# Giving out the first part of the last "back" between the last steps of the scans

## Chip, cores and metric

The program runs on one core of one Trainium2 chip. The time is the device time of that core in microseconds (us); lower is better. Three timed runs of the kernel before gave 13518.94, 13519.48 and 13551.32 us, so the median is 13519.48 us.

## What is computed

The input is a batch of 8 images of 64 channels and 64 x 64 positions, all in fp32. Four layers follow each other: an attention over all 4096 positions, two shifted-window attention blocks with their MLPs, a layer of position-dependent 3 x 3 filters with a convolution, and a state-space layer with four scan directions. Only the last layer bears on this change. Cut to what matters:

```
y  = out_y[:, 0] + inv[:, 0] + wh + invwh          # sum of the four scan directions
y  = _ln(y, outnorm_g, outnorm_b) * silu(z)        # over 128 inner channels
xh = xh + einsum("bhwd,cd->bhwc", y, outproj_w) + outproj_b
n  = _channel_ln(xh, cn_g, cn_b)
xo = xh + gelu(aggr(four dwconvs of n, three of them max-pooled by 2, 4, 8)) * n
```

Each direction is a recurrence over 4096 positions, `h = h * exp(dt * A) + dt * B * u`, for 128 channels and 16 states, followed by the sum over states of `h * C`.

## The kernel before

The images go through in four pairs, p = 0 to 3. `front(p)` computes the first three layers of a pair and the inputs of its scans and leaves them in DRAM. `scans(p)` (L1657) computes the scans, with the sums of the four directions written to DRAM. `back(p)` (L1808) reads these sums and does the rest of the last layer. `front` and `back` are Python generators: each `yield` gives up a piece of work with a cost. While `scans(p)` is written out step by step, it draws pieces of `back(p - 1)` and `front(p + 1)` in between, so these lie beside the scans. For the last pair, p = 3, only `back(2)` is left to lie beside its scans, and `back(3)` itself is run after everything, at L1930.

**The scans.** `scans` splits the work of a pair into 64 units: 2 images, 4 directions in the order k = 1, 3, 0, 2, and 8 blocks of 512 positions. A unit has 8 steps of two states each, so a pair has n = 512 steps. In step i, SP fetches B and C rows for later steps (`fetch`, L1720, 512 KB each, three buffers of each), POOL multiplies B by `dt * u` into `v` (`products`, L1725), ACT computes `exp(dt * A)` into a PSUM bank `dad` (L1747), DVE runs the two scans (L1750), and DVE or POOL multiply by C (L1765). For the last pair one of the two states of a step has its scan output left in PSUM and its C product done on DVE, in every fourth step both. PE adds the products into a PSUM bank with identity matmuls (`sums`, L1789). After the eighth step the bank is added into Y (L1799, L1801) and, in the fourth direction of an image, DVE forms the final sum of this block (L1804) and SP writes it to DRAM, tile `ys` (L1805). The fourth direction goes backward: its blocks are c = 7, 6, ..., 0. The tile of the final sum is the unit's own input tile `xs`, of which there are two, so the load of a later `xs` (L1697) waits for such a write.

**The back.** Its first part is a loop over the same blocks in the same order, c = 7 to 0, with three yields in each:

```python
for c in reversed(range(NCH)):
    po = self.bank("po3")
    for im in range(2):
        # load y (ys of this image) and z; normalise y:
        pc, sd = self.normed(...)          # PE pc, ACT square, PE pv, ACT ln, ACT exp
        # DVE u = pc * g * sd ; DVE u = (u + b) * z ; PE po[half] = opT @ u
        yield 6
    # DVE X = po + bias + X ; normed(X) ; DVE F = pc * g * sd ; ACT F = F + b
    yield 6
```

These are L1816 to L1833, with `normed` at L1231 to L1243. The two images share the partitions, so a block needs the sums of both: those of image 6 are finished halfway through the scans of p = 3, those of image 7 only in their last 8 units. The second part (from L1845) max-pools the whole of F three times, and then does the convolutions, the gelu and the output by blocks of 8 image rows. It needs all eight blocks of F.

**What sets the order.** Every engine has its own instruction queue, and the tile framework orders the instructions when it builds the program: it takes them by their place in the program text as soon as they can go, and gives buffers out in that order. PSUM banks come from two groups of three, "f" and "da". When `back(2)` has been used up during the last scans, `turn` is set (L1683), and from then on `bank` (L1209) alternates between the two groups for every request: the exponentials of the scans and the pieces of `back(3)` share all six.

Of the kernel before, what the change touches and what calls it, by code (L numbers as in the profile page):

```python
# [15 lines left out]
B, C, HH, WW = 8, 64, 64, 64  # L16
# [9 lines left out]
NTD = L // TD  # L26
# [1131 lines left out]
class _Direct:  # L1158
# [498 lines left out]
    def scans(self, p, beside, cost):  # L1657

        self.units = []
        for im in range(2):
            out = self.memory("ys")
            self.kept["y", 2 * p + im] = out
            for nth, k in enumerate((1, 3, 0, 2)):
                order = range(NTD) if k < 2 else range(NTD - 1, -1, -1)
                self.units += [dict(image=2 * p + im, k=k, c=c, at=at, nth=nth, out=out) for at, c in enumerate(order)]
        self.inputs(self.units[0])
        n = 8 * len(self.units)
        steps = [{} for _ in range(n)]  # L1670
        done = 0
        for i in range(-3, n):
            if i + 3 < n:
                self.fetch(i + 3, steps[i + 3], 0)
            if 0 <= i + 2 < n:
                self.fetch(i + 2, steps[i + 2], 1)
                self.products(i + 2, steps[i + 2])
            if i >= 0:
                self.step(i, steps[i])
                if i:  # L1680
                    self.sums(i - 1, steps[i - 1], steps[i]["w"])
                if p == B // 2 - 1 and done >= cost:
                    self.turn = max(self.turn, 0)  # L1683
                while done < cost * (i + 1) / (n - LEAD):
                    done += next(beside, cost)
            if i % 8 == 1 and i // 8 + 1 < len(self.units):
                self.inputs(self.units[i // 8 + 1])
        self.sums(n - 1, steps[n - 1])
        self.run(beside)

    def inputs(self, u):

        nc, w, net = self.nc, self.w, self.net
        wk, ps = self.sw, self.ps
        k, c = u["k"], u["c"]
        x = u["x"] = wk.tile([P, TD], F32, name="xs", tag="xs")
        nc.sync.dma_start(x, self.kept[u["image"]][k % 2][:, c * TD : (c + 1) * TD])  # L1697

        pd = ps.tile([P, TD], F32, name="pdd", tag="da")
        nc.tensor.matmul(pd, lhsT=net.xdt[:, k, :], rhs=x, start=True, stop=True)  # L1700
        du = u["du"] = wk.tile([P, 2, TD], F32, name="du", tag="du")
        nc.scalar.activation(
            pd, pd, AF.Exp, bias=w["dtb"][:, k : k + 1], accum_out=net.esum[:, u["image"], k, c : c + 1]
        )
        nc.scalar.activation(pd, pd, AF.Ln, bias=1.0)
        nc.vector.tensor_tensor(du[:, 1], pd, x, ALU.mult)
        nc.scalar.activation(du[:, 0], pd, AF.Copy)
        pb = ps.tile([2 * NST, TD], F32, name="pbc", tag="da")
        nc.tensor.matmul(pb, lhsT=w["xbc"][:, k, :], rhs=x, start=True, stop=True)
        bc = wk.tile([2 * NST, TD], F32, name="bc", tag="bc")  # L1710
        nc.scalar.activation(bc, pb, AF.Copy)
        rows = u["rows"] = self.dram.tile([2 * NST, TD], F32, name="rows", tag="rows")
        nc.sync.dma_start(rows, bc)
# [198 lines left out]
@with_exitstack  # L1912
def tile_kernel(ctx: ExitStack, tc: tile.TileContext, x: bass.AP, packs, layout, out: bass.AP):
    net = _Net(ctx, tc, x, packs, layout, out)
    with ExitStack() as path:
        net.open(path, True)
        d = _Direct(net, path)
        net.log_exp()
        front, first = d.begin(path)
        back = 0.25 * front  # L1920
        for p in range(B // 2):
            works, cost = [], 0
            if p:
                works.append(d.back(p - 1))
                cost += back
            if p + 1 < B // 2:
                works.append(d.front(p + 1))
                cost += front if p else front - first
            d.scans(p, d.chain(*works), cost)
        d.run(d.back(B // 2 - 1))  # L1930

    with tc.tile_pool(name="check", bufs=1) as pool:
        bad = net.in_range(pool)
    with tc.If(bad > 0), ExitStack() as path:
        net.open(path, False)
        for p in range(B // 2):
            t = net.layer0(p)
            t = net.layer1(t)
            t = net.layer2(t)
            net.layer3(t, p)  # L1940
# [21 lines left out]
```

## Time and profile before

| | us |
|---|---|
| median of three timed runs | 13519.48 |
| the profiled execution's own time | 13549.57 |
| its span | 13547.6 |
| the last pair's fourth direction of image 7: first and last final sum (L1804) | 13054.7 and 13293.1 |
| `back(2)`'s first part: first and last step of F (L1832) | 10957 and 11439 |

The profile is of one execution. It lies 30.1 us above the median, about where the slowest of the timed runs lies (13551.32 us). Sums are made against this execution and then set against the median. The span is 1.97 us shorter than the time of the execution; nothing in that remainder is touched. "Busy" in a table of stretches is the time in which at least one instruction of the engine ran, so instructions that overlap by a tenth of a microsecond are not counted twice. A wait is put down to whatever came last.

### The profile page before, as it was taken

To read this page: it belongs to the slowest core of one execution; us is meant where nothing else is said; L and a number is where in the kernel's file an instruction comes from. 1 tells how busy PE (TensorE), PEld (TensorE's weight loads), DVE (VectorE), ACT (ScalarE), POOL (GpSimd) and SP (SyncE) were. 2 spreads that over 40 slices of the span, in tenths; PEclk is the share of its full clock that TensorE was granted. 3 is DMA by queue.
4 is the path that set the end of the run, shared out by engine and by line. 5 is a ranking of instruction groups with operands and counts; after the bars stand their busy time and mean duration, and the time that the engine had idled before them with its cause. 6 is when DMAs were issued, how large, how long until landed. Compare 5 with 4: busy or idle time off the path is not lost. (4 is left out here: it accounts for less than half of the span.)

```text
span 13547.6 us, 140341 instructions
## 1 busy us (share of the span) xinstructions
PE 10802.4 (80%) x45762; PEld 3981.2 (29%) x45762; DVE 8783.4 (65%) x10407; ACT 7087.6 (52%) x15569; POOL 7764.9 (57%) x3875
## 2 busy tenths in 40 slices
PE   9999986888787669989888667997898666666665
PEld 2243322333232222224432222223443222222221
DVE  0121236776668676676666767667675768988985
ACT  5556514564545646655554545665653644544542
POOL 0000004887778764466666685446675687777881
PEclk9999977998898779999889788998888788888887
DMA  0000004776667765455555674455554677787882
GB/s 24 1 1 1 3 13 170 238 238 211 207 218 244 235 200 168 155 186 175 169 178 175 221 250 168 158 167 176 186 192 151 209 241 262 235 280 264 303 283 86
DMA packets 706249, 2385.12 MB, mean 176 GB/s; under 512 B 81120, under 2 KB 81248, under 8 KB 704480
## 3 DMA queue, kind: packets, MB, share of 16 engines
q1 hardware_dynamic: 681312, 2319.76, 50.9%
q10 hardware_dynamic: 24192, 56.29, 1.1%
q8 instruction: 362, 5.93, 0.2%
q14 instruction: 383, 3.14, 0.1%
HBM read 2272.97 MB, written 102.76 MB: 175 GB/s over the span
## 5 line engine op out<-in xcount | busy, mean ns | idle before, releaser
L1725 POOL TENSOR_TENSOR vd<-B,du 128x1024 f32<-128x1024 f32 x2048 | 4832.8, 2367 | 3924.8 <-DMA B<-rows 2573.0
L1789 PE MATMUL yd<-vd,pack 128*128 128x512 f32 x7540 | 4263.8, 696 | 1381.0 <-POOL vd L1761 591.9
L1747 ACT ACTIVATE dad<-du,As 128x512 f32<-128x512 f32 x4096 | 2729.0, 681 | 1130.8 <-DVE hd L1750 684.1
L1750 DVE TENSOR_TENSOR_SCAN hd<-dad,carry,vd 128x512 f32<-128x512 f32 x2166 | 2713.2, 1270 | 677.8 <-ACT dad L1747 385.9
L1789 PEld LDWEIGHTS yd<-vd,pack 128*128 128x128 f32 x7540 | 1497.0, 215 | 3843.5 <-issue 1654.4
L1761 POOL TENSOR_TENSOR vd<-hd,C 128x1024 f32<-128x1024 f32 x658 | 1551.4, 2358 | 1068.2 <-DVE hd L1750 702.0
L1750 DVE TENSOR_TENSOR_SCAN dad<-dad,carry,vd 128x512 f32<-128x512 f32 x1418 | 1793.3, 1274 | 160.3 <-POOL vd L1725 99.1
L1765 POOL TENSOR_TENSOR vd<-hd,C 128x512 f32<-128x512 f32 x1154 | 1476.1, 1280 | 512.5 <-DVE hd L1750 446.4
L1313 ACT ACTIVATE e<-s 128x512 f32<-128x512 f32 x2048 | 1200.7, 591 | 751.1 <-PE s L1307 749.6
L1307 PE MATMUL s<-X 64*128 64x512 f32 x4096 | 1344.4, 646 | 30.5 <-ACT e L1313 28.8
L1299 PE MATMUL po<-e,VT 128*64 128x512 f32 x4096 | 1226.7, 621 | 12.6 <-ACT e L1313 9.9
L1765 DVE TENSOR_TENSOR vd<-dad,C 128x512 f32<-128x512 f32 x1300 | 864.9, 672 | 48.2 <-ACT carry L1758 39.1
L1758 ACT ACTIVATE carry<-hd 128x1 f32<-128x1 f32 (+1 forms) x1586 | 317.3, 201 | 920.3 <-DVE hd L1750 917.0
L1758 ACT ACTIVATE carry<-dad 128x1 f32<-128x1 f32 x1422 | 240.9, 169 | 804.1 <-DVE dad L1750 801.4
L1307 PEld LDWEIGHTS s<-X 64*128 64x128 f32 x4096 | 375.9, 186 | 915.2 <-issue 783.1
L1447 DVE TENSOR_TENSOR w_e<-w_s,bias 128x512 f32<-128x512 f32 x512 | 329.9, 681 | 424.3 <-PE w_s L1435 423.6
L1462 PEld LDWEIGHTS w_av<-vals,w_e 64*64 64x64 f32 x16384 | 546.7, 144 | 197.3 <-issue 86.8
L1462 PE MATMUL w_av<-vals,w_e 64*64 64x9 f32 x16384 | 574.9, 207 | 30.4 <-ACT w_e L1452 30.1
L1700 PE MATMUL pdd<-xs,xdt 128*128 128x512 f32 x512 | 348.3, 768 | 257.8 <-DMA xs<-xc 121.4
L1452 ACT ACTIVATE w_e<-w_e 128x512 f32<-128x512 f32 x512 | 311.8, 626 | 366.9 <-DVE w_e L1447 251.6
L1299 PEld LDWEIGHTS po<-e,VT 128*64 128x64 f32 x4096 | 236.1, 135 | 847.5 <-issue 763.9
L1574 PE MATMUL acc<-tap,pack 128*128 128x512 f32 x576 | 367.5, 761 | 99.5 <-DVE tap L1573 98.1
(252 smaller groups left out, 11129.2 us busy)
## 6 DMA issues: line engine op xcount, KB each, us to landing
B<-rows SPq DMA_DIRECT2D x2048, 512.0 KB, 5.2
C<-rows SPq DMA_DIRECT2D x2048, 512.0 KB, 4.6
xs<-xt SPq DMA_DIRECT2D x128, 256.0 KB, 3.5
xs<-xc SPq DMA_DIRECT2D x128, 256.0 KB, 4.2
xc<-xcv ACTq DMA_DIRECT2D x64, 256.0 KB, 4.0
zs<-z ACTq DMA_DIRECT2D x64, 256.0 KB, 3.7
xt<-XT ACTq DMA_DIRECT2D x32, 512.0 KB, 7.8
rows<-bc SPq DMA_DIRECT2D x256, 64.0 KB, 1.6
```

The lines of the kernel that those rows point to most:

```text
L1299: nc.tensor.matmul(po[half[im]], lhsT=VT[:, t, half[im]], rhs=es[im], start=(t == 0), stop=(t == 31))
L1307: nc.tensor.matmul(ss[im], lhsT=at(half[im], t), rhs=X[half[im], jc * CH : (jc + 1) * CH], start=True, stop=True)
L1313: nc.scalar.activation(e, ss[im], AF.Exp, scale=C**-0.5, accum_out=parts[:, im, t, jc : jc + 1])
L1462: nc.tensor.matmul(self.av[half[im], x % 4 + j, h, :], lhsT=es[h // 4][half[im], j, h % 4, :], rhs=V[half[im], x + j, h, :], start=True, s ...
L1574: nc.tensor.matmul(acc, lhsT=w["ident"], rhs=tap, start=(t == 0), stop=(t == TAPS - 1))
L1725: self.nc.gpsimd.tensor_tensor(v, st["B"], dx.to_broadcast([P, 2, TD]), ALU.mult)
L1747: nc.scalar.activation(da, u["du"][:, 0], AF.Exp, scale=net.As[:, k, n : n + 1])
L1750: nc.vector.tensor_tensor_scan(along(to), along(da), along(v[:, j]), first, ALU.mult, ALU.add)
L1758: nc.scalar.activation(cs, ends, AF.Copy)
L1761: st["w"] = nc.gpsimd.tensor_tensor(v, h, CC, ALU.mult)
L1765: m = engine.tensor_tensor(v[:, j], hs[j], CC[:, j], ALU.mult)
L1789: m = nc.tensor.matmul(u["y"], lhsT=w["ident"], rhs=v, start=start, stop=stop)
```

## The change

`scans` makes the generator of `back(3)` itself, when it is at the last pair, and draws one piece of it after steps 3, 5 and 7 of every unit among the last seven (n - 8 * 7 = 456, so i = 459, 461, 463, ..., 511: 21 pieces, three for each of blocks c = 7 to 1). What is left of it, block c = 0 and the whole second part, runs after the last sum, as all of it did before. The call in `tile_kernel` goes away.

```diff
@@ in scans
         self.inputs(self.units[0])
         n = 8 * len(self.units)
+
+        late = self.back(p) if p == B // 2 - 1 else None
         steps = [{} for _ in range(n)]
@@
                 while done < cost * (i + 1) / (n - LEAD):
                     done += next(beside, cost)
+            if late and i >= n - 8 * (NTD - 1) and i % 8 in (3, 5, 7):
+                next(late)
             if i % 8 == 1 and i // 8 + 1 < len(self.units):
                 self.inputs(self.units[i // 8 + 1])
         self.sums(n - 1, steps[n - 1])
         self.run(beside)
+        if late:
+            self.run(late)
@@ in tile_kernel
             d.scans(p, d.chain(*works), cost)
-        d.run(d.back(B // 2 - 1))
```

Block c of image 7 is written one unit before the first piece of this block is drawn: unit c = 7 ends with i = 455, its final sum is written out with i = 456, and the pieces of block 7 come at i = 459, 461 and 463. No instruction is added or taken away: the number on each engine is the same, and so is everything computed.

## The prediction

> **What bounds the kernel now.** I read the table of stretches first, for the last two groups of units and for what follows them (columns: stretch, length, busy us and instructions of PE, PEld, DVE, ACT, POOL, clock, DMA share, GB/s).
>
> ```profile
> 12545.00:13005.00 460.00, 316.06 (x577) 106.63 (x576) 423.93 (x449) 235.50 (x561) 415.72 (x225) 0.90 0.88 304
> 13055.00:13285.00 230.00, 137.89 (x237) 45.32 (x238) 178.79 (x191) 96.99 (x229) 173.07 (x94) 0.85 0.72 257
> 13294.00:13458.00 164.00, 99.17 (x124) 26.90 (x122) 36.41 (x57) 48.70 (x79) 0.00 (x0) 0.66 0.14 45
> 13458.00:13547.60 89.60, 37.75 (x66) 15.01 (x66) 78.69 (x125) 16.07 (x22) 0.00 (x0) 0.69 0.07 25
> ```
>
> Row 1, other directions of image 7: DVE is busy 92% and POOL 90%. Row 2, the last direction: DVE is down to 78%, so there is room. Row 3, the last back's first part: PE 60%, ACT 30%, DVE 22%, POOL nothing. No engine is full there; the waits of this stretch tell why:
>
> ```profile
> PEld po L1827 <- DVE u L1826: 66.6, 16, 4.6
> ACT n_sd L1242 <- PE pv L1240: 66.4, 24, 6.7
> DVE u L1825 <- ACT n_sd L1243: 60.5, 16, 5.5
> DVE F L1832 <- ACT n_sd L1243: 50.5, 8, 6.3
> ```
>
> PE waits for DVE, ACT for PE, DVE for ACT, in turn: one dependent chain per block, 8 blocks. The timeline gives its start, the chain of waits its end:
>
> ```profile
> 13293.14 0.69 DVE L1804 TENSOR_TENSOR xs<-Y,yd 128x512 f32<-128x512 f32 x1 [2.63 <-PE yd L1789]
> 13293.86 0.32 SPq L1805 DMA_DIRECT2D ys<-xs  x1
> ...
> 13453.08 2.09 PE pv L1240 x2
> 13456.58 0.76 DVE F L1832
> 13458.12 2.29 DVE big L1845
> ```
>
> From the end of the last final sum, 13293.83, to the first instruction of the second part, 13458.12, it is 164.3 us.
>
> **What the Trainium skill says.** "PSUM — Partial Sum Buffer", section "Engine vs sequencer instructions": the queues of ScalarE, VectorE and GpSimd are strictly first in, first out, and matmuls go in program order. So a moved instruction that isn't ready holds up the scans queued behind it. The trace agrees: 60.5 us of DVE waiting stand at the head of its queue for L1825 alone. "SBUF — State Buffer", section "SBUF: two separate sides": a DVE operation with two SBUF inputs and a GpSimd operation exclude each other for the whole instruction. Of the back's DVE work only L1826 (u and z) is of that kind. The trace agrees, see its two durations below. "DMA: Bandwidth & Descriptors", section "Two DMAs through the same engine are not ordered": the reader of what a DMA wrote must wait for its semaphore before it is issued; the last block pays this below.
>
> **The change, part by part.**
>
> *Removed from the end.* Seven of the eight blocks leave it. What remains is block 0 after the last sum. Its chain, from the durations around 13304 us and the landings of the table of DMA issues: final sum ends 13293.8; ys write 2.0; yb read 2.7, with 0.3 for the two issues, 5.0; pc 2.1, square 0.6, pv 2.1, ln 0.7, exp 0.6, two u 1.5, po 1.4, X 0.75: 9.75; pc 2.1, square 0.6, pv 2.1, ln and exp 1.3, F 0.75, bias 0.7: 7.55. With hand-overs, some 0.1 at each of 15 steps, 1.5. Sum 23.8, taken as 24. Image 6's half of the block is ready early and hides beside it. The end becomes 164.3 − 24 = 140.3 us shorter. Block 1, whose last piece is written after the last step, must also be through; its ys lands one unit earlier, so I count nothing for it. The second part (89.6 us) is the same, only earlier.
>
> *Added to the last seven units.* The final sums go from 13054.7 to 13293.1, 238.4 us in 7 units, so 34.06 us each. Of block work each unit gets: PE 99.17 / 8 = 12.4 us (at a clock of 0.66; less at 0.85), ACT 48.70 / 8 = 6.1, DVE six instructions, SP four loads of 256 KB. What these cost beside scans is seen where `back(2)` lies beside scans, from 10900 to 11440 us:
>
> ```profile
> L1826 DVE SCALAR_TENSOR_TENSOR u<-u,pack,zb 128x512 f32<-128x512 f32 x15 | 21.5, 1433 | 0.2
> L1825 DVE SCALAR_TENSOR_TENSOR u<-pc,pack,n_sd 128x512 f32<-128x512 f32 x15 | 11.1, 738 | 29.8 <-ACT n_sd L1243 29.8
> L1832 DVE SCALAR_TENSOR_TENSOR F<-pc,pack,n_sd 128x512 f32<-128x512 f32 x8 | 5.9, 742 | 14.8 <-ACT n_sd L1243 14.8
> L1829 DVE SCALAR_TENSOR_TENSOR X<-po,pack,X 128x512 f32<-128x512 f32 x8 | 5.9, 739 | 4.0 <-PE po L1827 4.0
> ```
>
> L1826 is 1433 ns here and 752 ns in the end stretch, where POOL is idle. Per block DVE works 2 x 0.74 + 2 x 1.43 + 0.74 + 0.74 = 5.8 us, and waits at the head of its queue (29.8 + 14.8 + 4.0) / 8 = 6.1 us. What DVE has free now:
>
> ```profile
> DVE dad L1750 <- POOL vd L1725: 43.0, 25, 4.0
> DVE hd L1750 <- POOL vd L1725: 8.1, 8, 2.2
> ```
>
> That is 51.1 us in 230, or 7.6 us in a unit, spent waiting for POOL's product. Bounds on the growth of a unit: from below nothing, since 178.79 / 230 x 34.06 = 26.5 us of DVE work and 5.8 make 32.3, less than 34.06 (and less than nothing has no reason, no scan work goes away). From above 5.8 + 6.1 = 11.9 us, if no waiting is shared. In units 0 to 8 of the last pair (first L1706 at 11173.2, ninth at 11440.5) half a block lies beside a unit, which takes 33.4 us against 28.7 without one (row 1: 16 units in 460 us), so 4.7 more, or 9.5 a block. But there DVE has 8% free without the block, here 22%, and there the scans had three banks, here six less what the block holds. Two estimates lie between: if DVE gets as full as in row 1, some 90%, the unit is 32.3 / 0.9 = 35.9 us, growth 1.8; if all the block's DVE work comes on top, and only its waiting is shared with the waiting that is there now, growth is 5.8. I take the middle, 4 us: 7 x 4 = 28 us. Ends kept for the range: 0 and 7 x 11.9 = 83.
>
> *Added to queues.* PE: 20.4 us in a unit now (137.89 / 230 x 34.06) and at most 12.4 more, 32.8 of 38, in order; the sums wait a little longer behind pc and pv, which is covered by the six `v` buffers. ACT: 14.4 + 6.1 of 38. POOL: L1826 shuts it out for 2 x 0.75 us a block, inside the 22 to 25% that it has free. SP: four more issues, at 0.32 us each 1.3 us a unit, and y of image 7 waits for the ys write; but the next xs load already waits for this very write, so it is no new wait for the B and C fetches behind it. DMA: 1 MB on top of some 8.8 (34.06 us at 257 GB/s), share 0.72 to about 0.73 at the longer unit. All of these I take as nothing beyond the 4 us. If the cover of `v` is gone, POOL stops and the unit goes towards the upper bound.
>
> **Sum.** 13549.6 − 140.3 + 28 = 13437.3 for the profiled execution, a change of −112 us. From the median, 13519.5 − 112 = 13407 us, taken as 13408.
>
> **The rivals.**
>
> 1. *Wholly hidden.* The block fits in DVE's free time: 1 us a unit, 7 us, 13386 us. For it: 22% free and 32.3 < 34.06. Against it: DVE waited 6.1 us a block for ACT and PE in the earlier overlap.
> 2. *The chain is waited out in the queues.* As in units 0 to 8, 9.5 us a block: 67 us, 13446 us. For it: the earlier overlap did just this; po3 keeps a bank from step 3 to 7 and each pc one until u, so fewer of the six are left to run exponentials ahead. Against it: that stage was full, this one isn't.
> 3. *Slower.* Every one of the 21 pieces stalls DVE for a full chain, from pc at 13304.35 to the end of exp at 13310.58, 6.2 us, in units that have no free time to share, because the exponentials stand behind the square and ln on ACT and POOL behind DVE; with 5.8 us of work and a 5 us wait of SP for write and read in each unit, in front of the B fetches: 7 x (18.6 + 5.8 + 5) = 206 us, 13519.5 − 140.3 + 206 = 13585 us. It decides from 20 us of growth a unit on.
> 4. *It doesn't do what it says:* banks or buffers given out in program order hold the pieces back so that half of them still end after the last sum: 13460 us. `back(2)` argues against it: its blocks are interleaved with final sums of the pair before (F from 10957 us, last L1804 of that pair at 11170).
>
> **How the numbers follow.** Likeliest, growth 2 to 7 us a unit: 0.58, its own range 13393 to 13428. Rival 1: 0.17. Rival 2, 7 to 15 us: 0.18, of which 0.02 is within 0.3%. Rival 3: 0.04, of which 0.01 is within. Rival 4: 0.03, 0.01 of it within. A measurement of this kernel can tell about 0.3%, or 41 us, from no change. Faster 0.58 + 0.17 + 0.16 + 0.02 = 0.93, same 0.04, slower 0.03. The two levels of the runs before, 32 us apart, could show again and lift the median: 13408 + 32 lies inside. The range is 13375 to 13463: it leaves out the top of rival 2 and rival 3.
>
> **What would show it.** Right: one F row (L1832) per unit from about 13080 us on, final sums 36 to 41 us apart, the last final sum around 13320, the second part (L1845) 22 to 27 us after it, DVE at 85% or more in the last units with L1826 near 1.4 us. Wrong: final sums still 34 us apart (rival 1), 43 or more (rivals 2, 3), with DVE idle before L1825 and L1832; or more than two blocks of F after the last sum (rival 4). The forecast fails if the growth of a unit passes 12 us.

## The result: 0.64% faster, and the profile after

| | before | after |
|---|---|---|
| median of four timed runs, us | 13524.81 | 13438.59 |
| lowest and highest | 13518.94, 13551.32 | 13433.93, 13450.56 |
| the profiled execution's span | 13547.6 | 13435.7 |

The ratio is 0.9936, with a 95% interval from 0.9922 to 0.995: 86 us by the medians. The two spans lie 112 us apart, but that isn't the change alone. The order of instructions is the same up to the last direction of image 7, and there the profile of after is already 21.4 us ahead (its first final sum at 13033.3 us against 13054.7). From there on the account is this, each time read at the start of the instruction:

| us | before | after | difference |
|---|---|---|---|
| first to last of the eight final sums, 7 units | 238.4 | 291.4 | +53.0 |
| last final sum to the second part of the last back | 165.0 | 21.8 | −143.2 |
| second part to the last instruction | 89.4 | 89.1 | −0.3 |
| sum | | | −90.5 |

That fits the medians. How much the length of such a stretch differs from one profile to the next can be read from the 8 units just before, which no edit of this study aims at: from their first sum into Y to the first final sum it is 225.5 to 231.4 us in the thirteen profiles. Differences under some 5 us in the seven units are left unread below.

The stretches of the changed kernel (columns as before: stretch, length, busy us of PE, PEld, DVE, ACT, POOL, clock, DMA share, GB/s): the last seven units, the block that is left, the second part.

```profile
13033.00:13325.00 292.00, 203.95 (x359) 72.19 (x360) 222.87 (x240) 133.36 (x296) 176.12 (x94) 0.84 0.67 227
13325.00:13346.60 21.60, 11.10 (x18) 2.65 (x16) 6.07 (x18) 8.39 (x13) 0.00 (x0) 0.80 0.08 25
13346.60:13435.70 89.10, 37.85 (x66) 15.07 (x66) 78.67 (x125) 15.99 (x21) 0.00 (x0) 0.69 0.07 25
```

The same seven units before, from the same view:

```profile
13055.00:13293.00 238.00, 145.89 (x251) 48.58 (x252) 184.31 (x197) 97.58 (x230) 173.35 (x94) 0.85 0.70 250
```

DVE's busy time grew by 38.6 us, POOL's hardly (2.8 us), and DVE is 76% full in place of 77%. The added work did not fill the free time. What DVE now waits for (total us, times, longest):

```profile
DVE du L1712 <- ACT pdd L1711: 21.7, 5, 7.3
DVE vd L1771 <- DMA C<-rows: 8.7, 5, 3.2
DVE u L1831 <- ACT n_sd L1243: 7.9, 8, 1.5
DVE vd L1771 <- ACT carry L1764: 6.7, 6, 2.0
DVE hd L1756 <- POOL vd L1771: 6.3, 6, 1.7
```

The wait for POOL's product of B, 51.1 us before, is down to 3.7 us; with it stand many others, 68 us in all, the largest for the next unit's `du`. Only 7.9 us are waits for the block's own chain. But POOL and ACT wait for the block as well:

```profile
POOL vd L1771 <- DVE hd L1756: 36.0, 15, 5.5
POOL vd L1731 <- PE yd L1795: 27.7, 9, 3.8
```

```profile
ACT carry L1764 <- DVE dad L1756: 53.8, 47, 3.6
ACT n_sq L1238 <- PE pc L1236: 26.9, 11, 6.0
```

POOL waited 27.7 us for PE to read a `v` buffer, which it never did in the list of before. ACT stood 26.9 us with the block's square at the head of its queue and the exponentials behind it. What these waits cost the units can't be read from the lists; the experiments have to tell.

### The profile page after: what moved, and what is told of

Read it like the earlier page. It is cut to its first block, busy times and chain, and to the rows that moved or that the text cites. A ratio compares the mean times of both kernels' runs of the same rounds, so it can differ in the third digit from the quotient of the medians.

```text
span 13435.7 us, 140355 instructions
## 1 busy us (share of the span) xinstructions
PE 10771.7 (80%) x45762; PEld 3974.5 (30%) x45762; DVE 8806.3 (66%) x10407; ACT 7082.9 (53%) x15569; POOL 7764.7 (58%) x3875
## 5 line engine op out<-in xcount | busy, mean ns | idle before, releaser
L1706 PE MATMUL pdd<-xs,xdt 128*128 128x512 f32 x512 | 343.0, 757 | 236.8 <-DMA xs<-xc 102.8
```

## The experiments

Three causes were open: DVE's added work, the block's dependent chain standing in the queues, and the border between units (ys write, xs load, pdd, exp and ln, du), with PSUM banks and the port that DVE shares with POOL as smaller ones. All kernels were run three rounds beside the kernel before, in three sets with medians of before of 13541.14 (e1 to e4), 13511.93 (e5 to e8) and 13542.37 us (e9 to e11), so times are given as ratios. "Seven units" is always first to last final sum of image 7, read in the profile: 238.4 us before, 291.4 us in the changed kernel. Each kernel has one profile. By time alone, none of e1, e3 to e6 and e8 can be told from the changed kernel (their intervals overlap), so what is said of them rests on these stretches.

| kernel | seven units | DVE busy in them | ratio to before, 95% interval |
|---|---|---|---|
| the changed kernel | 291.4 | 222.9 | 0.9936, 0.9922 to 0.995 |
| e1: its sums in Y | 283.5 | 222.8 | 0.9927, 0.9911 to 0.9944 |
| e2: before, sums in Y | 217.0 | 183.7 | 0.9986, 0.9975 to 0.9996 |
| e3: po3 in its own bank | 280.1 | 211.8 | 0.9916, 0.9899 to 0.9933 |
| e4: no product with z | 271.4 | 200.8 | 0.9926, 0.991 to 0.9943 |
| e5: u in PSUM | 285.4 | 210.9 | 0.9913, 0.9896 to 0.9929 |
| e6: chain cut finer | 271.8 | 216.8 | 0.9934, 0.9915 to 0.9953 |
| e7: e3, e5, e6, all sums in Y | 255.0 | 209.9 | 0.9801, 0.9782 to 0.9819 |
| e8: no DVE work in the block | 264.7 | 184.0 | 0.9918, 0.9901 to 0.9935 |
| e9: e8 with e6 | 244.1 | 182.4 | 0.989, 0.9873 to 0.9906 |
| e10: e7 without the cut | 253.9 | 207.7 | 0.9779, 0.9763 to 0.9795 |
| e11: before, u in PSUM, all sums in Y | 213.9 | 184.0 | 0.986, 0.9839 to 0.988 |

**The border of a unit, e1 and e2.** Both form the final sum of image 7 in Y, so that the next xs load has no write to wait for.

```diff
-            o = u["x"]
+            o = self.Y[:, c * TD : (c + 1) * TD] if u["image"] >= B - 1 else u["x"]
             nc.vector.tensor_tensor(self.img(o), yd, yp, ALU.add)
```

> The changed kernel, but the final sums of image 7 are formed in Y itself and written to DRAM from there, so the load of the next xs no longer waits for this write. Border theory (DVE's idle time in the last units is the chain ys write, xs load, pdd, exp and ln, du at each unit's border, which the block's work can't fill): the last seven final sums, 41.6 us apart in the changed kernel, come 35 to 37 us apart, and the time falls by 30 to 45 us, to 13394 to 13409. Queue theory (the block's own chain, PE, ACT, PE, ACT, DVE, is waited out at the heads of the queues): 40 us or more apart, time within 10 us of 13439.

> The kernel before with the same edit: the final sums of image 7 formed in Y. Border theory: the last seven final sums, 34.06 us apart before, come 28.5 to 31 us apart, as the units of the other directions do (28.7), so the time falls by 21 to 39 us from 13525. If the idle time is not from the border: 34 us apart and within 10 us of before. Queue theory says nothing of this kernel.

In the kernel before it is as the border theory says: 217.0 us, 31.0 a unit (five of the seven 28.0 to 29.3), 21.4 us less, and the time of e2 agrees: 13522.34 us against 13541.14. PE's wait for the xs load, in the list of before and in that of e2:

```profile
PE pdd L1700 <- DMA xs<-xc: 25.0, 6, 5.6
```

```profile
PE pdd L1700 <- DMA xs<-xc: 9.2, 2, 5.0
```

In the changed kernel it isn't as that theory says: 283.5 us, 40.5 a unit, 7.9 us less. The idle time of DVE went elsewhere. Its waits and ACT's in e1:

```profile
DVE u L1831 <- ACT n_sd L1243: 32.0, 7, 9.3
DVE dad L1756 <- ACT dad L1753: 5.2, 3, 2.9
DVE hd L1756 <- ACT dad L1753: 4.8, 4, 1.8
```

```profile
ACT n_sq L1238 <- PE pc L1236: 60.7, 18, 10.3
ACT carry L1764 <- DVE dad L1756: 51.4, 45, 4.0
```

The wait at `du` is gone, and 32 us of waiting for the block's chain are there instead; ACT stands 60.7 us before the block's square. So the border was what DVE waited for in the kernel before, but it isn't what made the changed kernel's units grow: from e2 to e1 they grow by 66.5 us.

**The banks, e3.**

```diff
-                po = self.bank("po3")
+                po = self.total("po3") if p == B // 2 - 1 else self.bank("po3")
```

> The changed kernel with po3 of the last back in the one PSUM bank that lies unused then (tag acc), so that all six shared banks are left to the exponentials, pc and pv. Bank theory (po3 keeps one of six banks from step 3 to step 7 and holds the exponentials up): the growth of the last seven units, 53 us, falls by 20 us or more, time 13419 or less. Border theory and work theory: within 7 us of the changed kernel's units (41.6 us), time 13430 to 13448.

280.1 us: 11.3 less, between the two. That isn't the 20 us that would have made the bank the cause. By time the two can't be told apart (the intervals overlap). The DVE busy time is 11 us lower too, although this edit takes no DVE work away: its 14 instructions of L1832 take 979 ns on average, against 1551 in the changed kernel, 8.0 us together. So most of the gain may come from where these instructions fell beside POOL's, and not from the bank; no run tells the two apart.

**DVE's work, e4 and e8.** e4 leaves the second operation on u out of the last back, the gate's product. e8 leaves all of its DVE work in the first part out, and leaves the matmuls, loads and ACT work in.

```diff
-                    nc.vector.scalar_tensor_tensor(u, u, w["on_b"], z, ALU.add, ALU.mult)
+                    if p < B // 2 - 1:
+                        nc.vector.scalar_tensor_tensor(u, u, w["on_b"], z, ALU.add, ALU.mult)
```

```diff
-                    nc.vector.scalar_tensor_tensor(u, pc, w["on_g"], sd, ALU.mult, ALU.mult)
-                    nc.vector.scalar_tensor_tensor(u, u, w["on_b"], z, ALU.add, ALU.mult)
-                    nc.tensor.matmul(po[half[im]], lhsT=w["opT"], rhs=u, start=True, stop=True)
+                    if p < B // 2 - 1:
+                        nc.vector.scalar_tensor_tensor(u, pc, w["on_g"], sd, ALU.mult, ALU.mult)
+                        nc.vector.scalar_tensor_tensor(u, u, w["on_b"], z, ALU.add, ALU.mult)
+                    nc.tensor.matmul(po[half[im]], lhsT=w["opT"], rhs=u if p < B // 2 - 1 else y, start=True, stop=True)
...
-                nc.scalar.activation(d, d, AF.Identity, bias=w["cn_b"])
+                nc.scalar.activation(d, d if p < B // 2 - 1 else self.img(pc), AF.Identity, bias=w["cn_b"])
```

In e8 the operations that form X (L1835) and F (L1838) stand under the same condition.

> The changed kernel without the last back's second DVE operation on u (the product with z and its bias, L1832): the last pair's output lacks the gate. It takes 14 DVE instructions of 1.55 us out of the last seven units, 21.7 us, and shutting POOL out with them. Work theory (each us of DVE work in these units adds a us, as 38.5 of the 53 us of growth are DVE's busy time): the seven units get 18 to 25 us shorter together, 38.0 to 39.0 us each. Border or queue theory alone, with DVE not the bound: 0 to 8 us shorter together, 40.5 us or more each.

> The changed kernel without any DVE work in the last back's first part: po is formed from y, F is the bias and pc alone, X isn't updated by po; loads, matmuls and ACT work stay as they are, so the last pair's output is another. Work theory (DVE's 38.5 us of added busy time are the growth): of the 53 us of growth 0 to 17 stay, the units come 34 to 36.5 us apart. Queue theory on PE and ACT (the chain's links at the heads of their queues hold the scans up, whatever DVE does): 38 us or more.

e4: 271.4 us, 20.0 less, for 22.1 us less DVE busy time. This work cost nearly all of its time, although DVE is idle a quarter of the stretch. e8: 264.7 us, 26.7 less for some 39 us less DVE busy time, so 26.3 of the 53.0 us of growth stay with DVE's busy time at 184.0 us, as it was before. (The expectation of e9 below has 24 in place of 26.3: it counts to a wait of DVE at 13301.5 us, and the last final sum starts at 13303.5.) The work theory allowed 17. The queue theory asked for at least 28, which is missed by less than can be read, but it has no place for the 20.0 us of e4. So neither is enough alone. Both edits also take links out of the block's chain, so the DVE time and the shorter chain aren't told apart by them. The stretch of e8:

```profile
13038.80:13303.50 264.70, 194.72 (x361) 68.54 (x362) 184.00 (x198) 132.37 (x299) 173.71 (x94) 0.85 0.70 237
```

**The chain in the queues, e6 and e9.** The last back's `normed` becomes a generator, and its first part is drawn in nine pieces a block, so that each link stands a step behind the one that it waits for. e9 is e8 with the same cut.

```diff
+    def normed_by_parts(self, wk, src, cen, avg, eps):
...
+        nc.scalar.activation(sq, pc, AF.Square)
+        yield 2
...
+        nc.scalar.activation(sd, sd, AF.Exp, scale=-0.5)
+        yield 2
+        return pc, sd
...
-            if late and i >= n - 8 * (NTD - 1) and i % 8 in (3, 5, 7):
-                next(late)
+            if late and i > n - 8 * (NTD - 1):
+                next(late)
+                if i % 8 == 3:
+                    next(late)
```

> The changed kernel with the last back cut finer: nine pieces a block (pc and square; pv, ln and exp; the two u and po; and so on) drawn in every step of the last seven units, two in step 3, so that each link of the chain stands a step after the one that it waits for. Queue theory (in both kernels with the block some 61 to 70 us of DVE idle time stay in seven units, under other names each time, because links of the block's chain stand at the heads of PE's and ACT's queues before they are ready): the idle time of DVE falls to 35 to 50 us and the units to 37 to 39.5 us. Work theory alone: 41 to 42 us.

> The changed kernel without DVE work in the last back's first part (po from y, F from pc and the bias, X not updated by po; the last pair's output is another) and with the finer cut of e6. Of the 53 us of growth 24 stayed without DVE work. Queue theory (what stays is the chain's links standing at the heads of PE's and ACT's queues): the cut takes most of it, 10 us or less stay, units 34 to 35.5 us apart. Border theory for the rest (the four loads and the scheduler's order make the border of a unit longer, DVE waiting at du 30 us in e8): the cut doesn't matter, 17 to 31 us stay, units 36.5 to 38.5 us.

e6: 271.8 us, 19.6 less, inside what the queue theory gave for the units; DVE's idle time is 55 us (271.8 − 216.8), down from 68.5, which is less of a fall than it asked for. By time, 0.9934, e6 can't be told from the changed kernel. e9: 244.1 us, 20.6 less than e8, so that 5.7 of the 53.0 us of growth are left, about what can be read. Its stretch:

```profile
13076.00:13321.00 245.00, 185.63 (x362) 65.41 (x360) 182.43 (x199) 132.03 (x298) 173.91 (x94) 0.90 0.75 256
```

PE and ACT do all of the block's work here (185.6 and 132.0 us, against 145.9 and 97.6 before), and the units take it nearly for nothing once the links are spread out. The two causes add: 26.7 for DVE's work and 19.6 for the cut make 46.3, together they measured 47.3. The clock is a rival that no run excludes in full: the clock granted to PE was 0.90 in this stretch and 0.85 in e8's. In e6 the cut gave its 19.6 us at 0.86, against 0.84 in the changed kernel.

That the place of the links costs is shown by this; by which wait is not. Three waits of the seven units (us in total), from the lists of each run:

| kernel | seven units | POOL for PE to read `v` | ACT's square for pc | DVE at `du` |
|---|---|---|---|---|
| the changed kernel | 291.4 | 27.7 | 26.9 | 21.7 |
| e6 | 271.8 | 4.5 | 38.5 | 13.2 |
| e8 | 264.7 | 4.5 | 16.9 | 30.1 |
| e9 | 244.1 | 5.4 | 30.9 | 13.8 |
| e3 | 280.1 | 57.4 | 49.6 | 38.6 |

The cut makes ACT's wait for the square longer, not shorter, and POOL's wait for `v` is small in e8 already, where 26.3 us of growth stay. In e3 all three are longer than in the changed kernel and the units are shorter. Of the three only DVE's wait at `du` falls with the cut both times, by 8.5 and 16.3 us.

**The shared port, e5.** The first operation on u writes over pc in PSUM, in every back.

```diff
-                    nc.vector.scalar_tensor_tensor(u, pc, w["on_g"], sd, ALU.mult, ALU.mult)
-                    nc.vector.scalar_tensor_tensor(u, u, w["on_b"], z, ALU.add, ALU.mult)
+                    nc.vector.scalar_tensor_tensor(pc, pc, w["on_g"], sd, ALU.mult, ALU.mult)
+                    nc.vector.scalar_tensor_tensor(u, pc, w["on_b"], z, ALU.add, ALU.mult)
```

> The changed kernel, with the first DVE operation of every back (L1831) writing its result over pc in PSUM instead of into u in SBUF, so that the second (L1832) has one SBUF input and not two. Port theory (L1832 takes 1.55 us beside POOL and 0.75 without because the two shut each other out): L1832 falls to 0.75 to 0.85 us, 10 us less DVE time in the last seven units, and these get 8 to 12 us shorter together (40.0 to 40.5 us each). If the extra time is something else, L1832 stays above 1.3 us and the units at 41.6.

The view of this one line (ns: least, median, most) in the last seven units, first in the changed kernel, then in e5:

```profile
L1832 DVE SCALAR_TENSOR_TENSOR u<-u,pack,zb x14: 725/1652/2627, 13054.3 to 13319.2; 128x512 f32<-128x512 f32 x14
```

```profile
L1832 DVE SCALAR_TENSOR_TENSOR u<-pc,pack,zb x14: 725/748/752, 13009.6 to 13268.8; 128x512 f32<-128x512 f32 x14
```

With one SBUF input it takes its bare 0.75 us each time: what the port theory says of this instruction holds, and 12 us of DVE busy time go. The units get only 6.0 us shorter, under the 8 to 12 expected and hardly more than can be read. The ratio of the whole kernel, 0.9913, is lower than that of the changed kernel, but the intervals overlap.

**All of it together, e7, e10 and e11.** e7 has e3, e5, the cut of e6, and the final sums of all images in Y (the condition of e1 with 0 for B − 1). e10 is e7 with whole pieces. e11 is the kernel before with sums in Y for all images and u in PSUM.

> The cut of e6 with po3 in the bank of its own, u in PSUM and the final sums of all images formed in Y. If the gains add (8 us from Y, 11 from the bank, 10 from PSUM in the seven units, and 20 from the cut), the seven units take 240 to 255 us together against 291 in the changed kernel, and the other fourth directions get shorter too; the time is 13340 to 13400 on a chip where the kernel before takes 13525. If they are all one and the same idle time, the units stay near 39 us and the time at 13420.

> e7 with the three whole pieces a block of the changed kernel in place of the finer cut: po3 in its own bank, u in PSUM, final sums of all images in Y. If the cut is worth in this surrounding what it is worth in the changed kernel (19.6 us of 291), the seven units take 270 to 280 us (e7: 255) and the time is 15 to 25 us above e7's share of before, ratio 0.981 to 0.983. If the cut is worth nothing once the other edits are there: 255 us and ratio 0.980.

> The kernel before with final sums of all images in Y and u in PSUM, and the last back wholly after the scans. It tells what giving out the first part is worth in that surrounding. If a block costs a unit about what it did here (6 to 9 us, 40 to 65 us in all) against 140 us at the end, this kernel stands 75 to 100 us above e7, ratio 0.9855 to 0.988, with the last seven units at 210 to 220 us together as in e2 (217).

e7 takes 0.9801 and e10 0.9779 of the kernel before: 2.2% less, 13237.83 us against 13542.37 on its chip. e10 beats both kernels of this study. Most of it is none of the change's doing: e11, without the change, is at 0.986. The border between units costs in other fourth directions than the last, too: from first to last final sum, those of images 0, 1, 3, 5, 6 and 7 are 8 to 38 us shorter in e11's profile than before, those of images 2 and 4 aren't, and all eight together are 153 us shorter, of 211 us between the spans. Moving u alone, in e5, shortens none of the first seven by more than 9 us against the changed kernel. I had not foreseen this size and said 13340 to 13400 us for e7. The finer cut, worth 19.6 us in the changed kernel, is worth nothing here (255.0 and 253.9 us); DVE waits at `du` only 4.8 and 2.9 us in these two. In this surrounding the change is worth 101 us by the medians of e10 and e11, and 102 by their profiles: 163.8 − 21.7 = 142.1 us less at the end, 253.9 − 213.9 = 40.0 us more in the seven units. The stretch of e10:

```profile
12849.00:13103.00 254.00, 190.67 (x356) 63.87 (x356) 207.65 (x237) 129.71 (x295) 174.26 (x94) 0.90 0.79 261
```

## Why the forecast was right in kind and its gain 26 us too high, point by point

The forecast was −112 us and 13408 us; the medians say −86 us and 13438.6 us. The time lies inside the range, but outside the likeliest case's own (13393 to 13428), in rival 2's (7 to 15 us of growth a unit), at its lower edge. So the forecast was held by the width of its range as much as by its working: the likeliest case had about half of the growth, and rival 2 had named the queues.

- **The end gets shorter by 140.3 us: right.** 143.2 us were measured. From the end of the last final sum the left-over block took 21.1 us and not 24: pc and pv of y took 1.1 us each and not 2.1, at a granted clock of 0.80 in this stretch against 0.66 before. In the timeline of after, the wait for the ys write and the load of y stand where the forecast had them:

```profile
13324.76 0.69 DVE L1810 TENSOR_TENSOR xs<-Y,yd 128x512 f32<-128x512 f32 x1 [0.98 <-PE yd L1795]
13325.47 0.32 SPq L1811 DMA_DIRECT2D ys<-xs  x1
...
13327.52 0.32 SPq L1827 DMA_DIRECT2D yb<-ys  x1
...
13330.35 1.10 PE L1236 MATMUL pc<-yb,pack 128*128 128x512 f32 x2 [1.62 <-DMA yb<-ys]
...
13346.59 2.29 DVE L1851 TENSOR_TENSOR big<-F 128x2048 f32<-128x2048 f32 x1 [0.31 <-ACT F L1839]
```

- **The block's DVE work, 5.8 us a unit: right.** 38.6 us in seven units are 5.5. L1826 of before, now L1832, cost 1551 ns on average, forecast 1433, and e5 shows that its second SBUF input is why.
- **The growth of a unit, 4 us: the term that was mis-sized.** It measured 7.6 us, 53 in place of 28, and in the account of the two profiles that is the whole of the error. I took 4 as the middle between DVE getting 90% full and all its work coming on top. It was above that upper of the two estimates (5.8), and below the bound of 11.9. e4 and e8 show that most of the work's time did come on top (20.0 us for 22.1, 26.7 for 39). The reading "DVE is down to 78%, so there is room" is what misled: e2 shows that in the kernel before DVE was waiting out the latency of a unit's border.
- **PE and ACT "as nothing beyond the 4 us": the step that failed inside this term.** The forecast had the six `v` buffers cover the longer queue on PE. They didn't: POOL waited 27.7 us for them. But that wait isn't the cost itself, as it is 4.5 us in e8. e8 and e9 size the term: 26.3 us stay without any DVE work, and spreading the links takes 20.6 of these. PE was busy 74% and ACT 50% in e8's stretch, so neither was short of time; where the links stand in the queues was what cost, and by which wait stays open.
- **DVE waits 6.1 us a block for the chain: not at that place.** At L1831 it was 7.9 us in all seven units. DVE's other waits were for `du`, C, carries and exponentials; how much of them comes from the block's chain standing on ACT and PE isn't shown.
- **Rival 2's banks:** at most 11 us by e3, not the main cause. **Rival 4:** seven of eight blocks were done by 13329 us, as the change says. **Rival 3** would have needed 20 us a unit.
- **SP: no new wait, not quite.** It waited 9.8 us, two times, for a buffer of zb, and before the xs loads it waited 12.1 us for the ys writes, against 5.7 before. What this alone cost wasn't tried.
- **The earlier overlap, 9.5 us a block: read a little low.** The times 11173.2 and 11440.5 are those of the waits ahead of L1706; the instruction itself starts at 11173.8 and 11443.1, so a unit took 33.7 us and a block 9.8. The forecast's DMA share of 0.73 comes out as 0.72 from its own figures; 0.67 was measured.
- **The signs named in advance:** one F row a unit came true. The last final sum around 13320 (13324.8) came true by luck: this profile stood 21.4 us ahead when the units began. The second part came 21.8 us after it, just under 22 to 27. Final sums 36 to 41 us apart were 39 to 46 but for the last (30.6), four of the seven at 43 or more, which was half of the sign of rivals 2 and 3 (the other half, DVE idle before L1825, now L1831, was slight with 7.9 us); and DVE at 85% or more was 76%. These signs spoke against the sizing at once.

Still open is why the cut of the chain is worth 19.6 us in the changed kernel and nothing in e10, and which of e10's edits takes its place; only that they overlap is shown. The granted clock may have a part in this: it was 0.90 to 0.91 in the seven units of e7, e9 and e10, and 0.84 to 0.87 in those of all other kernels. Part of e10's 40.0 us of growth is also open: 23.7 us are DVE busy time (207.65 − 184.01), the other 16 were not taken apart.

## What to carry to other kernels

An engine's idle share in a stretch is not room for work: ask first what it idles on, since a latency that recurs in every unit (here a write that a load had to wait for, 21 us in seven units) need not fill up when work is added beside it. Price moved work at up to its full busy time on the fullest engine (here 0.9 of it in e4, 0.7 in e8, 0.5 in e5), and add a term for its dependent chain in the queues of the others, even where these have plenty of time. An earlier stretch of the same kernel with the same mixture (here 9.8 us a block, against 7.6 measured) was a better guide than a middle between bounds (4).

## What the runs showed of the hardware

One DVE operation of 128 x 512 fp32 with two SBUF inputs took 0.73 to 2.63 us beside POOL's products, and with one input moved to PSUM 0.73 to 0.75 us, over the same 14 instructions in the same place. Writing the intermediate into the PSUM bank that it was read from cost nothing that can be seen (0.758 us at the median for the first operation, 0.742 on average in the changed kernel).
